# A state-space scan with two products per step: one for GpSimd and one for VectorE in every step outside the dense attention

## The chip, the core and the metric

The kernel runs on one core of a Trainium2 chip. The metric is the device time of one execution in microseconds. TensorE (PE in the profile), VectorE (DVE), ScalarE (ACT) and GpSimd (POOL) each take their instructions in order from a queue of their own; SyncE (SP) issues most of the loads. All data are float32.

## What is computed

Four layers follow each other on x of 8 images, 64 channels, 64 x 64 positions: dense self attention over all 4096 positions with convolutions (layer 0), two window attention blocks with MLPs (layer 1), a filtered 3 x 3 convolution (layer 2), and a block whose core is a selective scan in four directions, followed by normalisation, gating and a small multi-scale convolution (layer 3). The change concerns the selective scan. Its reference, for 8 images, 4 directions k, 128 channels c and 16 states n:

```python
def step(h, inp):
    u_t, dt_t, B_t, C_t = inp
    h = h * jnp.exp(dt_t[..., None] * A) + dt_t[..., None] * B_t[:, :, None, :] * u_t[..., None]
    return (h, jnp.einsum('bkcn,bkn->bkc', h, C_t))
_, ys = jax.lax.scan(step, h0, (u, dt, Bl, Cl))
```

So every state n of every channel follows its own recursion over 4096 positions, and at each position the 16 states are multiplied with C and summed.

## The kernel before

Images are worked on in four pairs. `tile_kernel` runs `front` (layers 0 to 2 and the sources of the scan) for the first pair alone. Then, for each pair p, `scans(p, ...)` runs the scans of pair p, and beside them, mixed into the same queues, `back(p-1)` (the end of layer 3 for the pair before) and `front(p+1)`. The last pair has no front beside it, only `back(2)` and, late, its own `back(3)`.

**Units and steps.** A unit is one image, one direction and one chunk of 512 positions; a pair has 2 x 4 x 8 = 64 units. A unit has 8 steps, and a step handles two passes of 128 partitions (64 channels x 2 states each), j = 0 and 1, which the code and this text call its two states. There are 4 x 64 x 8 = 2048 steps. The two j have separate recursions.

**One step, i.** `fetch` loads the rows of B (three steps ahead) and of C (two ahead) through the SP queue. `products` (L1809, two steps ahead) makes v = B x du for both states in one GpSimd product of 1024 elements per partition. `step` then does for each j: ScalarE writes `da` = exp(dt x A) into a PSUM bank (L1831); VectorE runs the recursion over 512 positions as one scan instruction from `da`, `v` and the carry (L1834); ScalarE copies the scan's last element to `carries` for the next chunk (L1842, not in the last chunk of a direction). The scan's result is multiplied with C into v, in place. `sums` (L1860), two or three steps later, folds v on TensorE into the bank `yd` of the unit; after the eighth step `gather` (L1873 to L1878, VectorE) adds the bank to the output.

**Where the product with C goes.** `own` is the number of a step's products that VectorE makes.

- own = 0: both scans write the SBUF tile `h`, and GpSimd makes one product over both (L1845, 1024 elements). One copy moves both carries.
- own = 1: scan 0 writes `h` and GpSimd multiplies it (L1848, 512 elements); scan 1 writes over `da` in its PSUM bank, and VectorE multiplies that (also L1848).
- own = 2: both scans stay in PSUM and VectorE makes both products.

In the last pair (images 6 and 7), and in steps emitted while layer 0's dense attention of the next pair is being emitted (`self.dense`), four steps have own = 1, 1, 1, 2. In all others own is i % 2: even steps 0, odd steps 1.

**Buffers.** `dad`, `pdd` and `pbc` rotate through three PSUM banks (tag "da"), which in the last pair also serve half of what `back` needs. `v` has eight buffers of two states. `h` has two buffers of two states for even steps (tag h0) and two of one state for odd steps (tag h1).

**Order.** `scans` emits one step, then so much of the work beside it as its estimated costs (the numbers that `front` and `back` yield) make due, so steps are spread evenly over the work beside them in those costs. A scheduler then decides the order in each engine's queue when the kernel is built. The layer-0 attention that is called dense here is PE matmuls at L1324 and L1316 with exps at L1330; the window attention is L1411 to L1537 (`window_head`, `window_row`: scores on TensorE, bias on VectorE L1470, exp on ScalarE L1471, weighing on TensorE L1483 and L1494); its MLP is L1546 to L1560; layer 2's taps are VectorE products at L1619 between TensorE matmuls; the scan's sources are convolutions on TensorE (L1275) with L1674 to L1693; `back` is L1882 to L1991.

Of the kernel before, what the change touches and what calls it, by code (L numbers as in the profile page):

```python
# [9 lines left out]
F32 = mybir.dt.float32  # L10
AF = mybir.ActivationFunctionType
ALU = mybir.AluOpType
# [3 lines left out]
B, C, HH, WW = 8, 64, 64, 64  # L16
L = HH * WW
P = 128
# [6 lines left out]
TD = 512  # L25
NTD = L // TD
# [1133 lines left out]
class _Direct:  # L1160
# [650 lines left out]
    def step(self, i, st):  # L1811

        nc, w, net = self.nc, self.w, self.net
        wk, ps = self.sw, self.ps
        u = self.units[i // 8]
        k, c, at, CC, v = u["k"], u["c"], u["at"], st["C"], st["v"]


        n0 = 2 * (i % 8)
        own = 1 + (i % 4 == 3) if u["image"] >= B - 2 or self.dense else i % 2  # L1820
        rev = k >= 2

        def along(t):
            return t[:, ::-1] if rev else t

        h = wk.tile([P, 2 - i % 2, TD], F32, name="hd", tag=f"h{i % 2}", bufs=2)
        hs = []
        for j in range(2):
            n = n0 + j
            da = self.bank("dad", (P, TD), "da")  # L1830
            nc.scalar.activation(da, u["du"][:, j, 0], AF.Exp, scale=net.As[:, k, n : n + 1])  # L1831
            first = 0.0 if at == 0 else self.carries[:, n : n + 1]
            to = da if j >= 2 - own else h[:, j]
            nc.vector.tensor_tensor_scan(along(to), along(da), along(v[:, j]), first, ALU.mult, ALU.add)  # L1834
            hs.append(to)
            if at < NTD - 1 and (own or j):
                ends = h[:, :, 0] if rev else h[:, :, TD - 1]
                cs = self.carries[:, n0 : n0 + 2]
                if own:
                    ends = to[:, 0:1] if rev else to[:, TD - 1 : TD]  # L1840
                    cs = self.carries[:, n : n + 1]
                nc.scalar.activation(cs, ends, AF.Copy)  # L1842

        if own == 0:
            st["w"] = nc.gpsimd.tensor_tensor(v, h, self.twice(CC), ALU.mult)  # L1845
        for j in range(2 if own else 0):
            engine = nc.vector if j >= 2 - own else nc.gpsimd
            m = engine.tensor_tensor(v[:, j], hs[j], CC, ALU.mult)  # L1848
            st.setdefault("w", m)
# [193 lines left out]
```

## Time and profile before

| | us |
|---|---|
| median of 3 runs | 12007.1 |
| lowest, highest | 11998.7, 12011.9 |
| profiled execution | 12011.7 |
| its span, first to last instruction | 12009.9 |

| engine | busy us | share of the span |
|---|---|---|
| TensorE | 9980.9 | 83% |
| VectorE | 7806.3 | 65% |
| GpSimd | 7487.9 | 62% |
| ScalarE | 6974.8 | 58% |

Mean granted TensorE clock: 0.898 of full speed. The rows that follow are the page's strip of 40 equal slices of about 300 us; each digit is the busy share in tenths, PEclk the granted clock.

```profile
PE   9977999998888779998788978999877986675656
...
DVE  0033367767778474666777555666777748989998
...
POOL 0000066668778573666877774566778758888994
PEclk9998989999989889999998989999999987786677
```

The first five slices are the first pair's front alone: GpSimd does nothing. Then three periods follow, each with the dense attention (PE at 9), the window attention and layer 2, the convolutions, and a tail. From about 10000 us on the last pair runs. Busy shares of the whole span mix these stages; a stage is read from its own stretch. In a group's line, what stands after the second bar is idle time of that engine directly before the instructions of the group, and whose end ended it.

### The profile page before, as it was taken

The page shows a single profiled execution, that of the slowest core. Times are in us where ns is not written, and L with a number is a line of the kernel's source. Part 1 is how long each engine was busy: PE and PEld are TensorE (multiplying, and loading weights), DVE is VectorE, ACT ScalarE, POOL GpSimd, SP SyncE. Part 2 cuts the span into 40 slices and gives each one's busy share as a digit, 9 for nine tenths or more (in the row PEclk, how much of TensorE's full clock was granted, in tenths as well). Part 3 has the DMA queues.
Part 4 walks back from the last instruction along what each step waited for, and adds up shares of the span by engine and source line. Part 5 has one row for each costly group of instructions (what it writes and reads, how often), then busy time and mean ns, then how long its engine had stood idle before and what let it go on. Part 6 is the DMA issues. An engine that isn't in the chain of part 4 may idle for free. (4 is left out here: it accounts for less than half of the span.)

```text
span 12009.9 us, 161406 instructions
## 1 busy us (share of the span) xinstructions
PE 9980.9 (83%) x56180; PEld 3350.9 (28%) x56180; DVE 7806.3 (65%) x8943; ACT 6974.8 (58%) x16029; POOL 7487.9 (62%) x3843
## 2 busy tenths in 40 slices
PE   9977999998888779998788978999877986675656
PEld 2244322233322223223342223222333221121111
DVE  0033367767778474666777555666777748989998
ACT  5555367756665555665665554665666455565554
POOL 0000066668778573666877774566778758888994
PEclk9998989999989889999998989999999987786677
DMA  0000055545445553444444553444444446666663
GB/s 20 1 2 4 33 154 150 148 132 145 134 127 161 157 175 91 136 142 121 147 118 133 150 175 113 127 136 134 135 131 139 128 153 191 185 194 200 206 202 122
DMA packets 779773, 1577.04 MB, mean 131 GB/s; under 512 B 89280, under 2 KB 89408, under 8 KB 778176
## 3 DMA queue, kind: packets, MB, share of 16 engines
q1 hardware_dynamic: 736320, 1443.18, 40.2%
q10 hardware_dynamic: 42624, 123.44, 3.6%
q8 instruction: 444, 7.27, 0.3%
q14 instruction: 385, 3.15, 0.1%
HBM read 1197.16 MB, written 100.66 MB: 108 GB/s over the span
## 5 line engine op out<-in xcount | busy, mean ns | idle before, releaser
L1809 POOL TENSOR_TENSOR vd<-B,du 128x1024 f32<-128x1024 f32 x2048 | 4792.9, 2358 | 2802.6 <-DMA B<-rows 1797.4
L1860 PE MATMUL yd<-vd,pack 128*64 128x512 f32 x8192 | 2705.0, 705 | 668.8 <-POOL vd L1848 466.5
L1831 ACT ACTIVATE dad<-du,As 128x512 f32<-128x512 f32 x4096 | 2721.3, 682 | 697.0 <-DVE hd L1834 331.6
L1834 DVE TENSOR_TENSOR_SCAN hd<-dad,carry,vd 128x512 f32<-128x512 f32 x1989 | 2491.0, 1269 | 529.7 <-ACT dad L1831 471.4
L1848 POOL TENSOR_TENSOR vd<-hd,C 128x512 f32<-128x512 f32 x1293 | 1642.0, 1274 | 818.0 <-DVE hd L1834 816.8
L1834 DVE TENSOR_TENSOR_SCAN dad<-dad,carry,vd 128x512 f32<-128x512 f32 x1595 | 2011.5, 1276 | 184.4 <-ACT dad L1831 181.2
L1845 POOL TENSOR_TENSOR vd<-hd,C 128x1024 f32<-128x1024 f32 x488 | 1149.9, 2356 | 765.9 <-DVE hd L1834 362.7
L1330 ACT ACTIVATE e<-s 128x512 f32<-128x512 f32 x2048 | 1200.1, 591 | 623.4 <-PE s L1324 621.7
L1324 PE MATMUL s<-X 64*128 64x512 f32 x4096 | 1455.6, 647 | 85.5 <-ACT e L1330 66.0
L1848 DVE TENSOR_TENSOR vd<-dad,C 128x512 f32<-128x512 f32 x1827 | 1212.4, 677 | 130.0 <-ACT carry L1842 98.2
L1860 PEld LDWEIGHTS yd<-vd,pack 128*64 128x64 f32 x8192 | 617.5, 154 | 2403.4 <-issue 1152.3
L1316 PE MATMUL po<-e,VT 128*64 128x512 f32 x4096 | 1210.3, 627 | 19.3 <-ACT e L1330 16.2
L1842 ACT ACTIVATE carry<-dad 128x1 f32<-128x1 f32 x1597 | 267.1, 169 | 776.8 <-DVE dad L1834 684.0
L1324 PEld LDWEIGHTS s<-X 64*128 64x128 f32 x4096 | 400.6, 187 | 1129.3 <-issue 840.7
L1842 ACT ACTIVATE carry<-hd 128x1 f32<-128x1 f32 (+1 forms) x1559 | 308.8, 201 | 660.3 <-DVE hd L1834 649.4
L1483 PE MATMUL w_av<-wide,vals 64*32 64x64 f32 x16384 | 494.9, 227 | 116.6 <-DVE w_oc L1512 77.8
L1483 PEld LDWEIGHTS w_av<-wide,vals 64*32 64x32 f32 x16384 | 406.9, 113 | 272.2 <-issue 151.7
L1316 PEld LDWEIGHTS po<-e,VT 128*64 128x64 f32 x4096 | 235.7, 136 | 850.5 <-issue 570.8
L1243 PE MATMUL pv<-n_sq,pack 128*128 128x512 f32 x576 | 347.7, 687 | 148.8 <-ACT n_sq L1241 138.6
L1494 PE MATMUL w_av<-wide,each 64*32 64x128 f32 x8192 | 465.5, 282 | 6.6 <-issue 6.6
L1471 ACT ACTIVATE wide<-wide 128x512 f32<-128x512 f32 x512 | 311.5, 628 | 269.9 <-DVE wide L1470 269.9
L1339 DVE COPY att<-po 128x512 f32<-128x512 f32 x32 | 22.0, 686 | 682.8 <-PE po L1316 682.3
(259 smaller groups left out, 11629.5 us busy)
## 6 DMA issues: line engine op xcount, KB each, us to landing
B<-rows SPq DMA_DIRECT2D x2048, 256.0 KB, 3.6
C<-rows SPq DMA_DIRECT2D x2048, 256.0 KB, 3.6
du<-du SPq DMA_DIRECT2D x384, 512.0 KB, 5.8
du<-du ACTq DMA_DIRECT2D x128, 512.0 KB, 5.1
xs<-xt SPq DMA_DIRECT2D x128, 256.0 KB, 3.9
xs<-xc SPq DMA_DIRECT2D x128, 256.0 KB, 3.7
xc<-xcv ACTq DMA_DIRECT2D x64, 256.0 KB, 2.0
xt<-XT ACTq DMA_DIRECT2D x32, 512.0 KB, 6.1
```

Of the source, the lines that this page charges most:

```text
L1316: nc.tensor.matmul(po[half[im]], lhsT=VT[:, t, half[im]], rhs=es[im], start=(t == 0), stop=(t == 31))
L1324: nc.tensor.matmul(ss[im], lhsT=at(half[im], t), rhs=X[half[im], jc * CH : (jc + 1) * CH], start=True, stop=True)
L1330: nc.scalar.activation(e, ss[im], AF.Exp, scale=C**-0.5, accum_out=parts[:, im, t, jc : jc + 1])
L1483: nc.tensor.matmul(self.av[rows, 0, x % 4 + j], lhsT=net.vals[half[im], x + j, 4 * g + h], rhs=es[g][half[im], j, h], tile_position=(64 * ...
L1494: nc.tensor.matmul(self.av[rows, 1, x % 4 : x % 4 + 2], lhsT=net.each[half[im], 32 - HD - HD * h : 64 - HD - HD * h], rhs=es[g][half[im], ...
L1809: self.nc.gpsimd.tensor_tensor(v, self.twice(st["B"]), self.units[i // 8]["du"][:, :, 1], ALU.mult)
L1831: nc.scalar.activation(da, u["du"][:, j, 0], AF.Exp, scale=net.As[:, k, n : n + 1])
L1834: nc.vector.tensor_tensor_scan(along(to), along(da), along(v[:, j]), first, ALU.mult, ALU.add)
L1842: nc.scalar.activation(cs, ends, AF.Copy)
L1845: st["w"] = nc.gpsimd.tensor_tensor(v, h, self.twice(CC), ALU.mult)
L1848: m = engine.tensor_tensor(v[:, j], hs[j], CC, ALU.mult)
L1860: m = nc.tensor.matmul(u["y"][self.HALF[j]], lhsT=w["fold"], rhs=st["v"][:, j], start=(i % 8 == 0), stop=(i % 8 == 7))
```

## The change

Outside the last pair and the dense attention every step now has own = 1: even steps, which had own = 0, become like odd ones. The own = 1, 1, 1, 2 steps keep their rule. `h` is one state wide with four buffers for all steps. The double product and the double copy of the carry are gone.

```diff
-        own = 1 + (i % 4 == 3) if u["image"] >= B - 2 or self.dense else i % 2
+        own = 1 + (i % 4 == 3 and (u["image"] >= B - 2 or self.dense))
...
-        h = wk.tile([P, 2 - i % 2, TD], F32, name="hd", tag=f"h{i % 2}", bufs=2)
+        h = wk.tile([P, TD], F32, name="hd", tag="h", bufs=4)
...
-            to = da if j >= 2 - own else h[:, j]
+            to = da if j >= 2 - own else h
...
-            if at < NTD - 1 and (own or j):
-                ends = h[:, :, 0] if rev else h[:, :, TD - 1]
-                cs = self.carries[:, n0 : n0 + 2]
-                if own:
-                    ends = to[:, 0:1] if rev else to[:, TD - 1 : TD]
-                    cs = self.carries[:, n : n + 1]
-                nc.scalar.activation(cs, ends, AF.Copy)
-
-        if own == 0:
-            st["w"] = nc.gpsimd.tensor_tensor(v, h, self.twice(CC), ALU.mult)
-        for j in range(2 if own else 0):
+            if at < NTD - 1:
+                ends = to[:, 0:1] if rev else to[:, TD - 1 : TD]
+                nc.scalar.activation(self.carries[:, n : n + 1], ends, AF.Copy)
+
+        for j in range(2):
             engine = nc.vector if j >= 2 - own else nc.gpsimd
             m = engine.tensor_tensor(v[:, j], hs[j], CC, ALU.mult)
             st.setdefault("w", m)
```

In the built kernels, 488 GpSimd products of 1024 elements become 488 of 512 elements on GpSimd and 488 of 512 on VectorE; 488 more scans write PSUM instead of SBUF; 428 double copies of the carry become 856 single ones.

## The prediction

> **What bounds the kernel now.** I read the page's groups first, then cut the span into stages with the table of busy time by stretch, then asked in each stage what ended the waits around the instructions that are replaced. The page's groups price everything that is exchanged (busy us, mean ns of one, then the idle time just before it and its releaser):
>
> ```profile
> L1834 DVE TENSOR_TENSOR_SCAN hd<-dad,carry,vd 128x512 f32<-128x512 f32 x1989 | 2491.0, 1269 | 529.7 <-ACT dad L1831 471.4
> L1848 POOL TENSOR_TENSOR vd<-hd,C 128x512 f32<-128x512 f32 x1293 | 1642.0, 1274 | 818.0 <-DVE hd L1834 816.8
> L1834 DVE TENSOR_TENSOR_SCAN dad<-dad,carry,vd 128x512 f32<-128x512 f32 x1595 | 2011.5, 1276 | 184.4 <-ACT dad L1831 181.2
> L1845 POOL TENSOR_TENSOR vd<-hd,C 128x1024 f32<-128x1024 f32 x488 | 1149.9, 2356 | 765.9 <-DVE hd L1834 362.7
> ...
> L1848 DVE TENSOR_TENSOR vd<-dad,C 128x512 f32<-128x512 f32 x1827 | 1212.4, 677 | 130.0 <-ACT carry L1842 98.2
> ...
> L1842 ACT ACTIVATE carry<-dad 128x1 f32<-128x1 f32 x1597 | 267.1, 169 | 776.8 <-DVE dad L1834 684.0
> ```
>
> The 488 double products of L1845 are the steps that change. The table by stretch, one window for each kind of stage in the first pair's scans, and the last pair at the end (length, then PE, weight loads, DVE, ACT and POOL busy us, then the granted clock):
>
> ```profile
> 2680.00:3000.00 320.00, 264.82 (x4228) 126.44 (x4228) 250.85 (x301) 203.61 (x432) 262.27 (x129) 0.93 0.50 144
> 3400.00:3490.00 90.00, 65.36 (x160) 15.82 (x158) 65.48 (x72) 69.91 (x120) 78.18 (x39) 0.89 0.51 152
> 3500.00:3850.00 350.00, 299.96 (x833) 98.51 (x832) 270.19 (x309) 165.73 (x348) 278.11 (x137) 0.92 0.47 140
> 3850.00:4120.00 270.00, 230.43 (x531) 80.23 (x530) 104.70 (x109) 163.99 (x260) 150.78 (x74) 0.89 0.50 152
> 4120.00:4420.00 300.00, 205.93 (x446) 48.62 (x447) 238.03 (x248) 174.75 (x371) 272.90 (x136) 0.80 0.63 190
> 11000.00:11500.00 500.00, 298.77 (x662) 64.64 (x662) 486.14 (x517) 263.61 (x652) 474.86 (x258) 0.65 0.68 205
> ```
>
> In order: window attention, its MLP, layer 2, the scan sources, the tail (the steps beside `back`), the last pair. The last is plainly bound (VectorE 97%), and keeps its instructions. In window attention and layer 2 three engines stand near 80%, so busy time does not say which matters. The groups by stretch do; first the window attention (2680 to 3000), then the tail (4120 to 4420):
>
> ```profile
> L1860 PE MATMUL yd<-vd,pack 128*64 128x512 f32 x258 | 78.2, 633 | 15.5 <-POOL vd L1845 13.6 <-POOL vd L1848 1.2 <-DVE vd L1848 0.7
> L1845 POOL TENSOR_TENSOR vd<-hd,C 128x1024 f32<-128x1024 f32 x33 | 77.9, 2360 | 40.7 <-DVE hd L1834 32.3 <-issue 8.4
> ```
>
> ```profile
> L1860 PE MATMUL yd<-vd,pack 128*64 128x512 f32 x280 | 108.3, 781 | 37.9 <-POOL vd L1845 29.0 <-DVE xs L1878 6.0 <-POOL vd L1848 2.6
> ...
> L1845 POOL TENSOR_TENSOR vd<-hd,C 128x1024 f32<-128x1024 f32 x30 | 70.4, 2347 | 12.5 <-DMA C<-rows 9.5 <-issue 2.8 <-DVE hd L1834 0.2
> ```
>
> In window attention GpSimd idles 57.7 us of 320, and 40.7 of it lies before a double product, mostly until a VectorE scan ends: VectorE is late, GpSimd waits. In the tail hardly a product waits for a scan, and TensorE waits 29.0 us for double products. So load taken off GpSimd is worth something in the tails, and load put on VectorE costs something in the window attention.
>
> **The change, part by part.** Stage sums over all three pairs with a front beside them, from the same table (windows placed where each stage's lines run); L1845 counts in each:
>
> | stage | us | DVE | POOL | L1845 |
> |---|---|---|---|---|
> | window attention | 1720 | 1327 | 1301 | 159 |
> | layer 2 | 1080 | 799 | 819 | 101 |
> | MLP | 590 | 422 | 520 | 64 |
> | tails | 740 | 560 | 647 | 70 |
> | convolutions | 1180 | 525 | 666 | 78 |
>
> *Exchange of products.* For each changed step GpSimd drops 2356 ns and takes 1274 (saves 1082), VectorE takes a product of 677 and one scan writes PSUM instead of SBUF (1276 for 1269), together 684. Over 488: GpSimd -528 us, VectorE +334 us.
>
> *Window attention and layer 2.* VectorE gets (159 + 101) x 0.684 = 178 us. It is idle there for (1720 - 1327) + (1080 - 799) = 674 us, so between 0 (all falls into idle time) and 178 (none) reaches the end. VectorE's queue is in order, and the front's own loop runs through it: scores (PE), bias (DVE L1470), exp (ACT), weighing (PE); in layer 2 PE, taps (DVE L1619), PE. A product put before such an instruction delays the whole loop; one put where VectorE waits for the loop is free. In the 320 us window VectorE's waits are 67.6 us, 18.5 of them for `yd`, which a lighter GpSimd could shorten. I take 60%: **+107 us**. GpSimd falls there to 66%, which nobody feels, since it was the one that waited.
>
> *MLP and tails.* GpSimd is the fullest engine. MLP: GpSimd 520 - 64 x 1.082 = 451, VectorE 422 + 44 = 466; if the time followed the fullest engine, 590 x 466/520 = 529, 61 us less. Tails: 647 - 76 = 571 against 560 + 48 = 608; 740 x 608/647 = 695, 45 us less. Nothing gained is the other end, since VectorE becomes the fullest engine in both and the MLP holds it with waits for its second matmul (L1560, 12 to 23 us in each). I take half: **-53 us**.
>
> *Convolutions.* TensorE is 90% busy (1062 of 1180), both engines have room: 0, between -10 and +10.
>
> *Copies of the carry.* 488 x 7/8 = about 428 double copies become two; ACT gets 428 x 0.169 = 72 us. ACT is busy 64% in window attention; work of the other images covers it. Without cover in the MLP (ACT 75%) it costs 64 x 7/8 x 0.17 = 10 us. Taken as 0. Each added copy stands in ACT's queue waiting for its scan, with the next `exp` behind it and VectorE behind that; but the double copy already waited for the later of the two scans, so only the earlier wait is new. Priced with the banks below.
>
> *PSUM banks.* In a changed step the second state's bank stays taken through the copy and the product instead of falling free at the scan's end. Three banks rotate. Page rows: 366 waits of ACT for L1848, 0.86 us each. If all 488 added holds cost a full product and copy, 488 x 0.85 = 415 us; below nothing no reason points. The nearest row is the last pair, which holds banks so in every step and keeps VectorE at 97%. I take 0 and keep about 150 for the range.
>
> *Order.* The built order differs in all queues, also in the dense part, but every stage keeps its instructions; VectorE's typical order becomes scan, scan, scan of the next step, product. `h` has four single buffers where it had two double and two single ones, the same number of steps of lead. No DMA is added, removed or moved past a queue. Dense part and last pair: 0.
>
> Sum: 107 - 53 = +54 us on the profiled execution's 12011.7 us (span 12009.9 and 1.8 around it) is 12066; that execution lies 4.6 above the median of 12007.1, so 12061, rounded to **12060 us**.
>
> **Two rules of the skill.** The Trainium skill, GPSIMD Engine Reference, Engine selection, keeps two-input elementwise products on VectorE because GpSimd takes about twice as long. The rows: 1082 ns saved for 684 paid, 1.6. By the rule, engine time falls by 528 - 334 = 194 us and the kernel gets faster; by the rows it matters which queue is waited for, and in 2800 of these 5310 us it is VectorE's. Against the change speaks Perfetto Trace Analysis, Optimizing Scalar/DVE Operations: the two engines share an SBUF read port, so moving work between them might not help. If each added product locked GpSimd out, that would be 488 x 0.677 = 330 us on GpSimd. The rows: L1848 on VectorE, which reads one input from PSUM, takes 677 ns with GpSimd busy beside it, and the double product takes 2347 to 2360 ns in a tail as in window attention; I count none of it.
>
> **Rivals.**
> *B, GpSimd's relief wins (the other side).* It decides if more than about 85% of the added VectorE work falls into its waits in window attention and layer 2, because the double product, which must wait for both scans and then runs 2.36 us, is what `yd` (and VectorE's L1873 to L1878) waited for. Then +20 there, -106 in MLP and tails at the full scaling: about 11920; with part of either, 11900 to 11985. For it: 13.6 us of TensorE's waits above. Against: over all six window attention windows TensorE waits only about 26 us for products.
> *C, the two cancel,* 11985 to 12030.
> *D, the banks.* Waits of ACT for VectorE's products pass to the scans in the crowded stages: 54 + 150, about 12210. Against: in window attention VectorE waits 6 us of 320 for an `exp`.
>
> **The numbers.** A (above) 0.50, own range 12025 to 12165; B 0.30; C 0.13; D 0.07. 0.2% (24 us) is about what a measurement of this kernel can tell from no change: faster 0.30, same 0.13, slower 0.57. The range from 11925 to 12165 leaves out D and the lower edge of B.
>
> **What would show it.** L1845 gone; product rows on GpSimd x1781, on VectorE x2315 at about 677. Right if window attention and layer 2 grow by some 4% with VectorE at 84% and GpSimd near 66%, while MLP and tails shrink and TensorE's waits for `yd` there fall. Wrong if window attention keeps its length (B), or if VectorE's waits for `dad` <- ACT grow by more than 100 us (D), or if the dense part or the last pair changes length.

## The result and the profile after

| | before | changed |
|---|---|---|
| median, us | 12006.5 (11 runs) | 11978.3 (11 runs) |
| lowest to highest | 11998.7 to 12017.8 | 11962.9 to 11993.0 |
| ratio to before, 95% interval | | 0.9977 [0.9968, 0.9986] |
| span of the profiled execution | 12009.9 | 11961.1 |

The changed kernel is 28 us faster, 0.23%; 54 us slower was forecast. The profiled execution is the fastest of its eleven, so the two profiles differ by 49 us where the medians differ by 28; stage differences below are those of one profile each. As a measure of their scatter: in three kernels below that leave the tails as they were, tails and dense part together differ from before by -11 to +4 us.

The groups of the page that answer to those shown before (lines behind the change moved up by six, and both single products are now L1842):

```profile
L1842 POOL TENSOR_TENSOR vd<-hd,C 128x512 f32<-128x512 f32 x1781 | 2257.5, 1273 | 1919.8 <-DVE hd L1834 1896.1
...
L1834 DVE TENSOR_TENSOR_SCAN dad<-dad,carry,vd 128x512 f32<-128x512 f32 x2024 | 2562.5, 1278 | 243.1 <-ACT dad L1831 240.8
L1834 DVE TENSOR_TENSOR_SCAN hd<-dad,carry,vd 128x512 f32<-128x512 f32 x1560 | 1977.9, 1269 | 421.5 <-ACT dad L1831 384.0
L1842 DVE TENSOR_TENSOR vd<-dad,C 128x512 f32<-128x512 f32 x2315 | 1539.6, 677 | 174.9 <-ACT carry L1838 143.3
...
L1838 ACT ACTIVATE carry<-dad 128x1 f32<-128x1 f32 x2025 | 339.6, 169 | 931.5 <-DVE dad L1834 844.8
```

Every price of the exchange is as it was: 1273, 677, 1278, 169 ns. GpSimd waits 1896 us for scans before its products, where the two kinds of product before the change waited 1180. The same stages by stretch (window attention, MLP, layer 2, tail, last pair; PE, weight loads, DVE, ACT, POOL busy us):

```profile
2682.00:2981.00 299.00, 253.60 (x4157) 123.35 (x4155) 257.29 (x316) 194.72 (x437) 215.06 (x122) 0.95 0.50 145
3387.00:3479.00 92.00, 70.83 (x189) 18.17 (x190) 77.00 (x84) 78.59 (x137) 76.94 (x44) 0.91 0.57 171
3506.00:3798.00 292.00, 251.30 (x672) 82.23 (x673) 228.83 (x267) 124.08 (x277) 194.03 (x109) 0.90 0.45 132
4099.00:4419.00 320.00, 227.40 (x526) 64.62 (x524) 265.46 (x296) 189.01 (x430) 242.55 (x135) 0.83 0.58 175
10952.00:11452.00 500.00, 290.26 (x664) 63.35 (x664) 486.77 (x517) 261.83 (x651) 474.50 (x258) 0.67 0.67 205
```

VectorE is now the fuller of the two, or level with GpSimd in the MLP (77.0 and 76.9 us); in window attention it stands at 86%, and GpSimd has room. Yet the first window attention did not grow. Before, it took 307 us (first score bias to first MLP instruction):

```profile
2694.00:3001.00 307.00, 254.90 (x4162) 122.64 (x4156) 238.63 (x285) 193.66 (x410) 249.27 (x123) 0.92 0.49 143
```

It takes 299, with 18.7 us more VectorE work and nearly the same number of scans (121 for 120). VectorE's waits there (us, times, longest) show where the room came from; before:

```profile
DVE du L1789 <- ACT du L1777: 14.8, 5, 3.0
DVE X L1537 <- PE w_pp L1527: 12.2, 6, 2.4
DVE wsum L1511 <- ACT w_rc L1509: 12.0, 9, 2.6
DVE Y L1873 <- PE yd L1860: 9.9, 4, 2.6
DVE xs L1878 <- PE yd L1860: 8.6, 4, 2.7
```

and changed:

```profile
DVE du L1789 <- ACT du L1777: 14.8, 5, 3.0
DVE xs L1872 <- PE yd L1854: 7.0, 3, 3.6
DVE vd L1842 <- ACT carry L1838: 4.8, 11, 1.4
DVE wsum L1511 <- ACT w_rc L1509: 4.8, 5, 1.7
...
DVE X L1537 <- PE w_pp L1527: 3.3, 5, 1.6
```

All of VectorE's waits in that window fall from 67.2 to 40.5 us. Waits for the front (L1537, L1511) shrink to a third, and the waits for `yd` fall from 18.5 us (L1873, L1878) to 7.0 (L1872, which was L1878). A wait alone does not tell whether VectorE came later or the other engine was ready earlier; the experiments below separate the two sides. TensorE's matmuls and weight loads of `yd` show the other half. Before:

```profile
L1860 PE MATMUL yd<-vd,pack 128*64 128x512 f32 x242 | 73.2, 634 | 14.4 <-POOL vd L1845 12.6 <-POOL vd L1848 1.0 <-DVE vd L1848 0.7
...
L1860 PEld LDWEIGHTS yd<-vd,pack 128*64 128x64 f32 x242 | 15.5, 139 | 43.7 <-issue 21.2 <-POOL vd L1845 16.3 <-POOL vd L1848 2.6
```

Changed:

```profile
L1854 PE MATMUL yd<-vd,pack 128*64 128x512 f32 x243 | 75.2, 637 | 2.4 <-POOL vd L1842 2.4
...
L1854 PEld LDWEIGHTS yd<-vd,pack 128*64 128x64 f32 x244 | 16.3, 144 | 32.4 <-issue 24.3 <-POOL vd L1842 5.4 <-POOL vd L1809 1.7
```

In front of the `yd` matmuls 12 us of TensorE's waiting are gone (the weight loads wait for the same products; the two rows are not added).

Over all pairs, with stages marked by the first and last starts of their lines (two tails, three of the others), and the scans that ran in each:

| stage | before us | changed us | difference | scans before | scans changed |
|---|---|---|---|---|---|
| window attention | 1759.1 | 1785.7 | +26.6 | 656 | 674 |
| MLP | 626.0 | 568.4 | -57.6 | 269 | 250 |
| layer 2 with its lead-in | 971.2 | 995.4 | +24.2 | 358 | 364 |
| tails | 907.2 | 860.0 | -47.2 | 335 | 315 |
| dense attention | 2665.4 | 2686.1 | +20.7 | 1034 | 1054 |
| convolutions | 1385.6 | 1372.8 | -12.8 | 394 | 387 |
| last pair | 1999.2 | 2003.8 | +4.6 | | |

The scan columns warn against reading the differences singly. The built order moved 19 scans out of the MLP into its neighbours and 20 out of the tails into the dense attention. For the first tail and the dense part after it (length, VectorE busy in L1834 and its count), before:

```profile
4124.70:4577.80 453.10, 204.30 (x168) 0.85 0.52 157
4577.80:5442.90 865.10, 388.04 (x317) 0.98 0.44 128
```

changed:

```profile
4098.90:4518.70 419.80, 185.96 (x152) 0.87 0.51 154
4518.70:5402.10 883.40, 407.48 (x333) 0.98 0.45 132
```

Together both hold 485 scans and 1318 us before, 485 and 1303 after. So tails with dense part gained 26 us of the 47, and window attention, MLP and layer 2 together 7 us. That is what had to be explained: +107 us was forecast for window attention and layer 2, where the table has +51 with 24 more scans.

### The profile page after: what moved, and what is told of

It reads as the page before. It is cut to its first block, busy times and chain, and to the rows that moved or that the text cites. A ratio compares the mean times of both kernels' runs of the same rounds, so it can differ in the third digit from the quotient of the medians.

```text
span 11961.1 us, 162891 instructions
## 1 busy us (share of the span) xinstructions
PE 9975.9 (83%) x56180; PEld 3355.7 (28%) x56180; DVE 8083.6 (68%) x9431; ACT 7015.3 (59%) x16459; POOL 6975.2 (58%) x3843
## 5 line engine op out<-in xcount | busy, mean ns | idle before, releaser
L1809 POOL TENSOR_TENSOR vd<-B,du 128x1024 f32<-128x1024 f32 x2048 | 4801.5, 2360 | 2931.5 <-DMA B<-rows 1798.5
L1842 POOL TENSOR_TENSOR vd<-hd,C 128x512 f32<-128x512 f32 x1781 | 2257.5, 1273 | 1919.8 <-DVE hd L1834 1896.1
L1854 PE MATMUL yd<-vd,pack 128*64 128x512 f32 x8192 | 2662.4, 698 | 582.1 <-POOL vd L1842 519.5
L1834 DVE TENSOR_TENSOR_SCAN dad<-dad,carry,vd 128x512 f32<-128x512 f32 x2024 | 2562.5, 1278 | 243.1 <-ACT dad L1831 240.8
L1834 DVE TENSOR_TENSOR_SCAN hd<-dad,carry,vd 128x512 f32<-128x512 f32 x1560 | 1977.9, 1269 | 421.5 <-ACT dad L1831 384.0
L1842 DVE TENSOR_TENSOR vd<-dad,C 128x512 f32<-128x512 f32 x2315 | 1539.6, 677 | 174.9 <-ACT carry L1838 143.3
L1838 ACT ACTIVATE carry<-dad 128x1 f32<-128x1 f32 x2025 | 339.6, 169 | 931.5 <-DVE dad L1834 844.8
L1838 ACT ACTIVATE carry<-hd 128x1 f32<-128x1 f32 x1559 | 311.2, 200 | 761.5 <-DVE hd L1834 753.8
L1275 PE MATMUL xacc<-XI,diag 128*128 128x512 f32 x1024 | 465.7, 608 | 0.0
L1771 PE MATMUL pdd<-xs,xdt 128*128 128x512 f32 x512 | 334.9, 741 | 90.8 <-DVE vd L1842 49.1
```

The source lines that it names most:

```text
L1275: nc.tensor.matmul(dst, lhsT=diag[:, t], rhs=src, start=(t == 0), stop=stop and t == n - 1)
L1809: self.nc.gpsimd.tensor_tensor(v, self.twice(st["B"]), self.units[i // 8]["du"][:, :, 1], ALU.mult)
L1838: nc.scalar.activation(self.carries[:, n : n + 1], ends, AF.Copy)
L1854: m = nc.tensor.matmul(u["y"][self.HALF[j]], lhsT=w["fold"], rhs=st["v"][:, j], start=(i % 8 == 0), stop=(i % 8 == 7))
```

## The experiments

Theory 1 is the prediction's stage picture with another size: outside window attention and layer 2 GpSimd's relief pays, inside VectorE's load costs something, less than forecast. Theory 2: the gain is one of the built order or of `h`. Each run's ratio is to the kernel before on the same chip; "heavy" in the edits is window attention and layer 2 of the front as it is emitted.

**By stage.** Two kernels that split the change. The flag is set when window attention or layer 2 is emitted, and cleared by the MLP and the scan's sources.

```diff
-        own = 1 + (i % 4 == 3) if u["image"] >= B - 2 or self.dense else i % 2
+        own = 1 + (i % 4 == 3) if u["image"] >= B - 2 or self.dense else i % 2 if self.heavy else 1
```

> The kernel before, with one product per engine in every step except in the window attention and layer 2 (and the dense attention and the last pair, as in both kernels): 209 of the 488 double products are exchanged, those beside the MLP, the tails and the convolutions; 279 stay. Theory 1 (stage by stage: MLP and tails follow the fullest engine, window attention and layer 2 pay for VectorE's added work): the MLP and tail gains of the changed kernel (-58 and -47 us in the profile) come and the +47 us of window attention and layer 2 do not: 80 to 110 us faster than before, so faster than the changed kernel by some 50. Theory 2 (the gain is one of the built order, or of h, and belongs to no stage): about 209/488 of the changed kernel's 28 us, so 12 us faster than before.

Measured: 11962.5 against 12001.6 us, 0.9967 [0.9955, 0.9979]: 39 us faster. The complement has `1 if self.heavy else i % 2`:

> The complement: one product per engine only in the window attention and layer 2; 279 double products exchanged, 209 stay. Theory 1: window attention and layer 2 some 47 us longer, MLP and tails as before: 30 to 50 us slower than before. Theory 2: 279/488 of 28, about 16 us faster than before.

Measured: 12016.3, 1.0014 [1.0005, 1.0023]: 15 us slower. The signs are theory 1's and the sum of the two, -24, is the changed kernel's -28; both are about half of what the profile's stage differences led me to expect, since those double count the scans that moved. Theory 2, a gain that belongs to no stage, falls for the sign; an effect of the order within a stage is not ruled out by it. The third kernel of this kind keeps the double products beside the MLP as well (the line that clears the flag there is left out):

> As the earlier run that spares window attention and layer 2, but the MLP keeps the double products as well: exchanged are only the steps beside the tails and the convolutions, 162 of 488. Theory 1 as predicted (MLP and tails each follow the fullest engine): the MLP's share of 35 to 58 us is lost, so 0 to 15 us faster than before. Theory M (the MLP's windows were long in the kernel before by the built order, since every reordered kernel shortened them, also the ones that left the products there alone): most of that run's 39 us stays, 25 to 45 us faster.

Measured: 11982.3, 0.9984 [0.9975, 0.9994]: 19 us faster. So the MLP is worth 20 us, tails and convolutions 19; the total lies between the two theories. The MLP itself decides: with its products untouched it took 622.4 us in this run (626.0 before), so theory M falls, and the MLP gains by the exchange. But 16 scans leave it in the first kernel (253 for 269), and of the 48 us by which its windows shrink there some 27 come back in window attention and layer 2, which leaves about the 20 of the medians.

**Load and relief apart.** One kernel gives VectorE the work and leaves GpSimd's double product:

```diff
             st["w"] = nc.gpsimd.tensor_tensor(v, h, self.twice(CC), ALU.mult)
+            nc.vector.tensor_tensor(da, da, CC, ALU.mult)
```

> The load on VectorE alone: the kernel before keeps its double products, and after each of the 488 VectorE makes one more product of 512 elements that nothing uses (it overwrites the PSUM bank of the second state with its product with C, so it holds the bank as the change does). Theory 1a (what window attention and layer 2 absorbed fell into VectorE's own waits for the front): there +50 us as in the changed kernel; MLP and tails gain nothing and pay up to 90: in all 50 to 140 us slower. Theory 1b (the load was paid for by the double product's going, whose lateness VectorE and TensorE waited for): window attention and layer 2 alone +110 us or more, in all 150 to 250 us slower.

Measured: 12109.5, 1.0086 [1.0073, 1.0100]: 108 us slower, with the added row at 678 ns x488, 330.8 us. The other relieves GpSimd and gives VectorE nothing:

```diff
-            st["w"] = nc.gpsimd.tensor_tensor(v, h, self.twice(CC), ALU.mult)
+            st["w"] = nc.gpsimd.tensor_tensor(v[:, 0], h[:, 0], CC, ALU.mult)
```

> The relief of GpSimd alone: in the 488 steps GpSimd multiplies only the first state with C (512 elements for 1024) and the second state's product is left out of the computation, so VectorE gets nothing. Theory 1a: MLP and tails fall by about 105 us as in the changed kernel or a little more, window attention and layer 2 stay within 15 us: 100 to 130 us faster than before. Theory 1b: window attention and layer 2 fall by 60 us or more as well: 165 us or more faster.

Measured: 11955.1, 0.9958 [0.9945, 0.9972]: 47 us faster, less than half of what either theory said. Load and relief add to +61, the exchange is -28: together they are better than their sum, so both were split by stage. Load only in window attention and layer 2 (the added line of the first kernel under `if self.heavy:`):

> The load on VectorE alone, only in window attention and layer 2: the kernel before with one idle product more on VectorE (in place on the second state's bank) in the 279 even steps there, the double products kept. This is the price that the prediction put at 60% of 0.684 us a step. Theory 1 (VectorE's waits take it up by themselves): 15 to 45 us slower than before (under a quarter of 279 x 0.678 = 189 us). Theory 1b (only with GpSimd relieved do they): 80 us slower or more.

Measured: 12071.7, 1.0055 [1.0041, 1.0069]: 68 us slower, 36% of 189. It lies between the two theories. Relief only outside (the single product under `if not self.heavy:`):

> The relief of GpSimd alone, only outside window attention and layer 2: in 209 even steps beside MLP, tails and convolutions GpSimd multiplies the first state only, and the second state's product with C is left out of the computation. Theory 1 (there the fullest engine is GpSimd, as predicted): at least what the exchange brings there, 40 us or more faster than before. Theory 2 (the exchange gains there by something else than GpSimd's load): less than half of it, 0 to 20 us faster.

Measured: 11972.1, 0.9972 [0.9961, 0.9982]: 31 us faster, between the two theories, and four fifths of what the exchange brings there. But it does not come from the same stages. In this run's profile the MLP is 16 us shorter (609.6 us, with 271 scans for 269), while tails and dense part together are not shorter at all: 3575.7 us for 3572.6, with the same scans. The first tail before, then in this run, then this run's matmuls there:

```profile
4124.70:4577.80 453.10, 351.14 (x844) 116.53 (x844) 306.84 (x336) 221.72 (x471) 318.96 (x160) 0.85 0.52 157
4090.60:4550.10 459.50, 355.69 (x846) 118.88 (x846) 303.60 (x336) 223.24 (x471) 288.42 (x160) 0.83 0.50 155
L1863 PE MATMUL yd<-vd,pack 128*64 128x512 f32 x330 | 121.5, 714 | 18.5 <-POOL vd L1851 8.9 <-POOL vd L1848 4.9 <-DVE xs L1881 4.1
```

GpSimd has 31 us less to do, TensorE's waits before these matmuls fall from 37.9 to 18.5 us, and the tail still takes 459.5 us for 453.1. The relief everywhere shows the same (-2 us for tails and dense part). Relief only inside:

> The relief of GpSimd alone, only in window attention and layer 2: in the 279 even steps there GpSimd multiplies the first state only, and the second state's product with C is left out of the computation. It closes the square of load and relief in these two stages. The prediction took this relief at nothing: within 10 us of before. If load and relief add up there, the exchange's +15 us less the load's +68 leaves it 53 us faster. By the difference of the relief everywhere and the relief outside (-47 and -31) it is 15 us faster; between these two, what is missing from 53 is worth something only with VectorE loaded.

Measured: 11963.2, 0.9968 [0.9957, 0.9979]: 42 us faster. In its first window attention (2690 to 2990 us, nearly the same window as above) TensorE's waits for `yd` show part of it:

```profile
L1863 PE MATMUL yd<-vd,pack 128*64 128x512 f32 x243 | 76.6, 638 | 7.0 <-POOL vd L1848 5.4 <-POOL vd L1851 0.9 <-DVE vd L1851 0.7
```

7.0 us for 14.4. Three things come together here: the product is shorter, it starts after the first scan instead of the second (one starts at 2731.25 us, while VectorE's scans run on to 2733.5), and TensorE's fold of the second state waits for no product with C, since that product is left out. They were not separated. In this run's profile the six window attentions are 26.6 us shorter with the same 656 scans, and layer 2 keeps its length (970.7 us for 971.2). The MLP, whose products are as before, is 28.7 us shorter with 10 scans fewer, and the convolutions, with 10 more, are 11.1 longer. The square, in us against before:

| | neither | load | relief | both | load + relief |
|---|---|---|---|---|---|
| window attention and layer 2 | 0 | +68 | -42 | +15 | +26 |
| elsewhere | 0 | +40 (108 - 68, not run) | -31 | -39 | +9 |

Inside, load and relief add up within the intervals. Outside they do not, if the difference of two runs may stand for the load.

**What else the exchange carries.** The double product cut in two, both on GpSimd:

```diff
-            st["w"] = nc.gpsimd.tensor_tensor(v, h, self.twice(CC), ALU.mult)
+            st["w"] = nc.gpsimd.tensor_tensor(v[:, 0], h[:, 0], CC, ALU.mult)
+            nc.gpsimd.tensor_tensor(v[:, 1], h[:, 1], CC, ALU.mult)
```

> The kernel before, with each double product of GpSimd cut into two single ones, one per state, both still on GpSimd (one launch more, about 190 ns in each of 488 steps, 93 us of GpSimd); nothing goes to VectorE. Theory G (what the exchange brings beyond load and relief is that the first product need not wait for the second scan): 20 to 50 us faster than before in spite of the launches. Theory B (the balance between the two engines alone): no gain, 0 to 40 us slower.

Measured: 12044.3, 1.0037 [1.0022, 1.0051]: 43 us slower. An early start of the first product is no gain that shows; 93 us more on GpSimd cost 43. The page's two groups of this kernel:

```profile
L1845 POOL TENSOR_TENSOR vd<-hd,C 128x512 f32<-128x512 f32 x488 | 621.5, 1274 | 444.4 <-DVE hd L1834 440.9
...
L1846 POOL TENSOR_TENSOR vd<-hd,C 128x512 f32<-128x512 f32 x488 | 621.5, 1274 | 132.1 <-DVE hd L1834 128.3
```

Twice 1274 ns stand where 2356 stood. The changed kernel with the old buffers of `h`:

```diff
-        h = wk.tile([P, TD], F32, name="hd", tag="h", bufs=4)
+        h = wk.tile([P, 2 - i % 2, TD], F32, name="hd", tag=f"h{i % 2}", bufs=2)
...
-            to = da if j >= 2 - own else h
+            to = da if j >= 2 - own else h[:, 0]
```

> The changed kernel with the buffers of h as before (two of two states for even steps, of which half is used, and two of one state for odd steps). Theory 1 (h is only bookkeeping): as the changed kernel, 20 to 40 us faster than before. Theory H (four single buffers in one rotation let the scans run further ahead and are the source of the gain): the gain goes, within 10 us of before.

Measured: 11968.4, 0.9971 [0.9961, 0.9982]: 33 us faster, as the changed kernel. `h` is bookkeeping. Last, the exchange with VectorE reading the second state from SBUF:

```diff
-            st["w"] = nc.gpsimd.tensor_tensor(v, h, self.twice(CC), ALU.mult)
+            st["w"] = nc.gpsimd.tensor_tensor(v[:, 0], h[:, 0], CC, ALU.mult)
+            nc.vector.tensor_tensor(v[:, 1], h[:, 1], CC, ALU.mult)
```

> The exchange with the second state in SBUF: in the 488 steps both scans write h, GpSimd multiplies the first state and VectorE the second, which it reads from h instead of from a PSUM bank; so the bank falls free at the scan's end, and VectorE's product has both inputs in SBUF. Theory P (banks or port do not matter): as the changed kernel, 20 to 40 us faster than before, both engines' rows of the products within 2% of 677 and 1273 ns. Theory S (two SBUF inputs contend with GpSimd for the shared port): the rows of either engine grow by hundreds of ns, and the kernel is slower than before by 50 us or more.

Measured: 12205.6, 1.0172 [1.0158, 1.0186]: 204 us slower, theory S. The groups of its page:

```profile
L1849 POOL TENSOR_TENSOR vd<-hd,C 128x512 f32<-128x512 f32 x1293 | 1704.4, 1322 | 1499.1 <-DVE hd L1834 1490.3
...
L1849 DVE TENSOR_TENSOR vd<-dad,C 128x512 f32<-128x512 f32 x1827 | 1206.0, 673 | 140.5 <-ACT carry L1842 109.3
...
L1845 POOL TENSOR_TENSOR vd<-hd,C 128x512 f32<-128x512 f32 x488 | 650.8, 1334 | 585.1 <-DVE hd L1834 567.4
...
L1846 DVE TENSOR_TENSOR vd<-hd,C 128x512 f32<-128x512 f32 x488 | 637.2, 1306 | 2.0
```

The same product of 512 elements takes VectorE 673 ns with one input in PSUM (L1849) and 1306 with both in SBUF (L1846; 656 at the least, 2866 at the most), and GpSimd's products grow by 4 to 5%.

**A version between.** Inside window attention and layer 2 the exchange in every second even step only (`(i % 4 > 0) if self.heavy else 1`):

> One product per engine outside window attention and layer 2, as in the run that spares these two, and inside them in every second of the even steps only: 139 of the 488 double products stay. Theory 1 (VectorE's added work there is nearly all taken up by its waits, and GpSimd's relief there brings nothing): between the run that spares them and the changed kernel, 25 to 40 us faster than before. Theory K (both engines stand at the knee there, and the best share lies between): faster than either, 45 us or more.

Measured: 11969.2, 0.9970 [0.9959, 0.9982]: 35 us faster, between the two; no share between them showed up as better. The median furthest from before, among the kernels that leave nothing out, is the first one's, -39 us with the exchange outside window attention and layer 2 only; its interval and the changed kernel's overlap.

## Why the prediction was wrong, point by point

*The exchange of products* held: the rows are 1273, 677 and 1278 ns, the counts 1781 and 2315. GpSimd's busy time fell by 513 us (528 worked out). VectorE's rose by 277 (334): its product row alone rose by 327, but in the trace instructions back to back on VectorE overlap by about 0.1 us, and busy time counts that once. Taken together the two engines have 236 us less to do (194 worked out, from the rows); that sum had the sign of the result right, but only 28 us of it reached the end.

*Window attention and layer 2, "I take 60%: +107 us"*, is the step that failed; it was +15 in the run that changes only these. Two terms of it were wrong. The load's share that reaches the end was 36%, measured by itself (68 of 189 us, 279 steps), not 60%. And "GpSimd falls there to 66%, which nobody feels, since it was the one that waited" was false: the relief alone was worth 42 us there. That GpSimd waits before its product says only that it is not behind at that moment; the double product starts when the later scan ends, and its length then stands between that scan and TensorE. A single product of 1274 ns in place of 2356 halved TensorE's waits for `yd` in the first window attention (7.0 us for 14.4), and in the changed kernel they are 2.4. The prediction had this in its rival B and set it aside because TensorE's matmuls waited only 26 us for products in all six windows. Those 26 do not cover the 42 either. By the profiles 27 us of the relief's gain lie in window attention, where TensorE's matmuls wait 13 us less for products (7.7 for 21.0), and none in layer 2. What gave the rest, and how much of the 42 is the shorter product rather than its earlier start or the left-out second product, was not settled.

*MLP and tails, "I take half: -53 us"*: about the size, -39 for everything outside window attention and layer 2, of which the MLP 20. In the MLP the mechanism is supported: GpSimd's relief alone shortened it by 16 us with 2 scans more. (Kernels that left its products alone moved it too, to between 597 and 623 us, the short ones with 6 to 10 scans fewer.) VectorE still waits 71 us for L1560 in its six windows (103 before), which may be what kept it from the full 61; that was not tested. In the tails the mechanism failed and the size was luck: GpSimd's relief alone shortened nothing there (+3 and -2 us with the dense part), although TensorE's 29.0 us of waiting for double products, from which the prediction argued, was shortened. Only the kernels with the whole exchange there gain.

*Convolutions, copies of the carry*: no effect that stands out. The convolutions are 13 us shorter with 7 scans fewer; ACT is 40 us busier.

*PSUM banks, taken as 0*: right. VectorE's waits for the `exp` of the four kinds of scan fell from 722 to 689 us, so rival D is out. ACT's waits for VectorE's products rose from 314 to 377 us, and its waits for `hd` scans fell from 332 to 127.

*The shared port, none counted*: right for a product that reads PSUM. With both inputs in SBUF the price would have been 488 x (1306 - 677) = 307 us of VectorE, and the kernel slower by 204. The Trainium skill, SBUF - State Buffer, section SBUF: two separate sides, states it: a VectorE instruction with two SBUF inputs and a GpSimd instruction that reads SBUF exclude each other for a whole instruction. The trace agrees. One such product starts at 2725.55 us, while GpSimd is in a product of L1809 from 2724.74 to 2727.09, and ends only at 2727.63, 2.08 us long; GpSimd's next product, begun at 2727.05, takes 1.72 us for the usual 1.27. The longest VectorE product of L1846, 2866 ns, exceeds the shortest, 656, by 2210, less than one L1809 product (2355).

*Dense part and last pair, 0*: the last pair held (+5). The dense part took 20 scans over from the tails in the changed kernel, and in the four other kernels that have the exchange beside the tails and were counted (the first, the one without the MLP, the one with the old `h`, the one between; 1054 scans in each), but not in those with GpSimd's relief alone or with the double product cut in two (1034 in each; 1038 where VectorE read SBUF). With the exchange beside the tails, tails and dense part together are 19 to 32 us shorter in all five kernels; with the relief alone they are not shorter. So this is where the exchange gets much of the 48 us by which, elsewhere, it beats load plus relief. Whether the new order gives them, or VectorE's product itself, was not separated. That stays open, as does the load alone outside window attention and layer 2, which was not run.

*The rivals*: B came nearest. It had GpSimd's relief at work in window attention and layer 2, and the net there (+15 measured, +20 said), and the time lies in its band for a part of either. Its condition, that more than 85% of the added work falls into VectorE's waits, did not hold for the load by itself (64%); only net of the relief does 8% (15 of 178 us) reach the end. And it gave MLP and tails their full 106.

## What to carry to other kernels

An engine that waits before an instruction is not thereby off the path: after the wait, the length of that instruction still stands in front of whoever needs its result, so shortening it can pay although the engine has idle time. That GpSimd's relief paid in window attention is measured; that it paid by this length is the reading that fits best. The reverse also holds: in the tails here the fuller engine got lighter and the wait for it shorter, and the time stayed. When work moves from one engine to another, measure load and relief apart and by stage; here each alone was larger than the exchange. Before reading a stage as faster or slower, count the units of work that ran in it, because a rebuilt order moves work over the stage's edges.

## What the runs showed of the hardware that was not expected

The same VectorE product, 128 x 512 float32, took 673 ns with one input in PSUM and 1306 ns on average with both in SBUF beside a busy GpSimd. A GpSimd product of 1024 elements took 2356 ns and two of 512 took 2 x 1274, so by this estimate each instruction carries about 190 ns whatever its length; 93 us more of it in this kernel came with 43 us more time, although GpSimd is idle for 38% of the span.
